# A list scheduler's rules and constants are rewritten, and a whole program is put in a new order

## The chip, the core and the metric

The kernel runs on one core of a Trainium2 chip. The core's engines each run their own queue of instructions in order: TensorE (PE in the profile, with its weight loads shown apart as PEld), VectorE (DVE), ScalarE (ACT), GpSimd (POOL) and SyncE (SP, which only issues DMAs here). An instruction that needs a value from another engine waits for a semaphore, and everything behind it on its own queue waits with it. The metric is device time in microseconds (us), from one launch to its end.

## The reference

A batch of 32 elements, each a 256 x 256 block in fp32, goes through four layers, one after another. Cut to what matters:

```
x = layer_0(x, t)        # conditioning vectors from t; two whole-block norms, silu, two 256x256 products, residual
x = layer_1(x, mask, timestep, bias)
    # norm, scale and shift; 16 heads of width 16: softmax(q k^T / 4 + bias, mask) v
    # output product, norm, 256 -> 1024 -> 256 feed-forward with x * sigmoid(1.702 x)
x = layer_2(x, A, B, dt) # finite differences along both axes of A*x and B*x, x + dt * df, max(., 0)
x = layer_3(x, gate)     # norm, 16 causal heads of width 16, feed-forward with exact gelu, gated residual
```

The attention bias alone is 32 x 16 x 256 x 256 floats; it is what the kernel mostly loads (512 DMAs of 256 KB).

## The kernel before

Each batch element is one block of 128 partitions x 2 x 256. Nothing depends on another batch element, so the work of several elements can be mixed on the engines: while one element is in its layer 3, the next is in layer 1 and the one after in layer 0.

The code of a layer does not issue instructions. `Order.record` only notes every operation with its operands, its nominal time `order.now`, and a cost from `Order.length`. `trace` sets the nominal time: element b's layer i starts at `b * PERIOD + START[i] + EDGE[b, i]`, each `yield` of a layer moves it on by that step's size times `PACE[i]`, and `SHIFT[i]` moves single steps to and fro. When all is recorded, `arrange` plays the program through on a model of the five engines: at each moment it gives every free engine the ready unit with the lowest rank (the nominal time, for PE less `EARLIER` of its tile's kind). The start times that come out are not used as times. `emit` issues all instructions sorted by them, so the model sets only the order of each queue; semaphores do the rest on the chip. As all instructions are issued by one line of `emit`, the profile names that line, L365 (`call(*args, **kwargs)`), for every one of them, and groups have to be told apart by their tiles.

What the model counts, in `length` and `arrange`:

- the length of each operation by engine, method and elements a partition (the pair returned is the time until its result is there and the time until the engine is free);
- `HOPS` and `OWNS`: from an operation's end to the start of a dependent one on another engine and on its own; `SLACK` is added where the dependent one is on PE;
- on PE, three array shapes: full 128x128, 32 rows x 128 (scores, tile `sc`: heads of width 16 in slots of 32 rows) and 128 x 32 columns (the products with the values, tile `pt` into `mm`). Each change of shape costs `TURN`, the first product of a slot `FIRST`, and `SEEN` is when a result counts as landed;
- a port that DVE and POOL are taken to share: an operation marked `x["port"]` starts only after the other engine's marked one is done;
- PSUM: eight banks, of which `CAPS` lets at most so many be used by scores (`sc`), transposed probabilities (`tr`) and everything else (`mm`).

PE works on six kinds of units: full fp32 products (256 columns; two records in the profile for each), transpositions through the identity (`ident`, one record), mean products of one column (`mean_mat`), stencil products of 129 columns, scores and value products. A unit of `order.together()` stays in one piece.

The steps that the prediction follows: `values` multiplies the transposed probabilities with V into `mm` and ACT copies it to `ctx_t`; `inverse_sums` has POOL spread the reciprocals of the softmax sums into `wide`; `normalise` has PE transpose `wide` and DVE multiply `ctx_t` by it; the product `ctx_t` x `L1wo` follows. `token_norm` has DVE take the statistics `st` and `mv`, `rstd_of` has POOL compute `rstd` (two small instructions, the second a power), DVE computes `shift` from it (128 x 2 elements), and ACT writes the normalised tile `t`, which PE transposes. POOL's largest work is `nb`: 512 subtractions of the attention bias from the mask, 16 for an element.

Of the kernel before, what the change touches and what calls it, by code (L numbers as in the profile page):

```python
# [21 lines left out]
P = 128  # L22
# [19 lines left out]
PERIOD = 86.0  # L42
START = (-59.8, 0.0, 116.9)
PACE = (1.37, 1.22, 1.08)
EDGE = {(0, 0): -102.4, (0, 1): -3.5, (0, 2): 0.3, (1, 0): -29.2, (1, 1): -9.5, (1, 2): -3.3, (2, 0): -4.4, (2, 1): -1.3, (2, 2): 1.9, (3, 0): 7.5, (3, 2): 0.7, (4, 0): -2.3, (4, 1): 1.2, (4, 2): 0.6, (27, 0): 7.3, (27, 1): 1.5, (27, 2): 0.7, (28, 0): -2.3, (28, 1): 1.6, (28, 2): 4.6, (29, 0): 2.1, (29, 1): -0.7, (29, 2): -0.1, (30, 0): 0.1, (30, 1): 3.4, (30, 2): -0.3, (31, 0): 3.1, (31, 1): 3.6, (31, 2): -30.9}
SHIFT = (
    {0: -23.5, 1: -31.5, 2: -24.4, 3: -36.5, 4: -13.4, 5: -35.7, 6: -44.8, 7: -28.5, 8: 20.9},
    {0: -11.9, 1: -93.5, 2: -5.9, 3: 2.4, 4: 4.1, 5: 6.4, 7: -9.2, 8: 7.3, 9: -92.1, 11: 7.2, 12: 20.9,
     13: -0.6, 14: 4.6, 15: -3.0, 16: 12.9, 17: 7.8, 19: 5.4, 20: 7.9, 21: 35.0, 22: 16.8, 23: -7.6,
     24: -11.1, 25: -25.5, 26: -3.5, 27: -66.1, 28: -0.5, 29: -110.6, 30: -4.3, 31: -15.2, 32: -19.4,  # L50
     33: 1.6, 34: -0.4, 35: 12.9, 36: 0.6, 37: -15.0},
    {0: -3.0, 1: -43.2, 2: 3.0, 3: 26.5, 4: 23.8, 5: -31.8, 6: -42.4, 7: -14.5, 8: -8.2, 9: 6.5,
     11: 3.8, 12: 16.4, 13: -29.4, 15: -3.4, 16: 18.0, 17: -4.1, 18: 7.0, 19: 0.1, 20: 0.7, 21: -69.9,
     23: 8.3, 24: 7.8, 25: -0.5, 26: -13.8, 27: -43.4, 28: 14.4, 29: -5.3, 30: 25.3, 31: 1.7, 32: -8.7,
     33: -40.0, 34: 13.4, 35: -21.0, 36: -92.3, 37: -36.5, 38: -60.7, 39: 56.2, 40: -26.9, 41: 7.7},
    {0: -11.5, 1: 3.4, 2: -31.6, 3: -95.1, 4: 57.5},
# [8 lines left out]
class Order:  # L65
# [9 lines left out]
    HOPS = {"act": 40.0, "dve": 40.0, "pool": 90.0, "pe": 60.0, "sync": 60.0}  # L75
    OWNS = {"act": 30.0, "dve": 30.0, "pool": 83.0, "sync": 30.0}
    TURN = 92.0
    FIRST = {(32, P): 107.0, (P, 32): 27.0}
    SLACK = 50.0
    SEEN = 165.0  # L80
    CAPS = {"sc": 6, "tr": 7, "mm": 6}
    EARLIER = {"sc": 28.7, "mm": -1.9, "tr": 6.1}
    STAY = 5.0
    PORT = 0.05
# [41 lines left out]
    def record(self, engine, call, method, args, kwargs):  # L126
# [12 lines left out]
        inner = [a for a in ins if math.prod(n for _, n in a.ap[1:]) >= 16]  # L139
        sources = sum(a.space != PSUM for a in inner)  # L140
        alone = method in ("tensor_scalar", "tensor_copy") and all(a.space != PSUM for a in outs)
        x["port"] = bool(inner) and (engine == "pool" or engine == "dve" and (sources > 1 or sources == 1 and alone))
# [25 lines left out]
    def length(self, engine, method, outs, ins, args, kwargs):  # L168
# [5 lines left out]
        if engine == "pe":  # L174
            lhs = kwargs.get("lhsT")
            rows = 32 if lhs is not None and lhs.partition_size() <= 32 else P
            cols = 32 if outs[0].partition_size() <= 32 else P
            slot = (lhs.start_partition(), outs[0].start_partition()) if lhs is not None else (0, 0)
            passes = 1 if method == "transpose" or kwargs.get("is_transpose") else 2
            one = max(free(outs[0]) / 1.2 + 2.3, 109.0) if free(outs[0]) > 16 else 70.0  # L180
            return one * passes, (rows, cols), slot
        if method == "dma_start":
            return sum(math.prod(k for _, k in a.ap) for a in outs) * 4
        if engine == "dve":
# [3 lines left out]
            if method == "tensor_tensor_reduce":  # L188
                return 235 + 1.05 * n, 73 + 1.05 * n, lead
# [3 lines left out]
            elif method == "scalar_tensor_tensor":  # L193
                a = 205 + 1.05 * n
                lead = 195.0
            else:
                a = 148 + 1.05 * n
            return a, a - 80, lead
        if engine == "act":
            if method == "copy":  # L200
                a = 157 + 0.84 * n
            else:
                a = (255 if columns else 200) + 0.84 * n + (93 if columns > 1 else 0)
                if "accum_out" in kwargs:
                    a += 115
            return a, a - 95, self.TABLES.get(args[2] if len(args) > 2 else None)
        if method == "tensor_tensor":
            a = 640 if n <= 4 else 185 + 2.13 * n
        else:
            a = 185 + 0.86 * n + (70 * columns if columns > 1 else 0)  # L210
        return a, a - 40 if n > 4 else a + 10

    def arrange(self):
# [48 lines left out]
        table = None  # L262

# [12 lines left out]
        while todo:  # L276
# [6 lines left out]
            for e in self.ENGINES:  # L283
# [6 lines left out]
                for k, heap in ready[e].items():  # L290
# [5 lines left out]
                    if e == "pe" and units[u][2][0]["length"][1] != shape:  # L296
                        rank += self.STAY
                    if k[1]:
# [11 lines left out]
                for x in units[u][2]:  # L310
                    if e == "pe":
                        one, its_shape, slot = x["length"]
                        if its_shape != shape:
# [7 lines left out]
                        done = t + one + (0.0 if slot in slots else self.FIRST.get(shape, 0.0))  # L321
# [3 lines left out]
                        done += self.SEEN  # L325
# [4 lines left out]
                    else:  # L330
                        x["start"] = now
                        more = max((pool_end if e == "dve" else dve_end) - now - x["lead"], 0.0) if x["port"] else 0.0
                        more = max([more] + [t - now for f, t in map(banks.__getitem__, x["banks"]) if f != e])
# [3 lines left out]
                        done, t = (now + a + more for a in x["length"][:2])  # L337
                        if x["port"] and e == "pool":
# [848 lines left out]
```

## Time and profile before

| what | number |
|---|---|
| median of 3 runs | 2708.8 us (2708.65 to 2711.2) |
| profiled execution, its own time | 2711.45 us |
| its span, first to last instruction | 2709.7 us |
| granted TensorE clock, mean over the span | 0.988 |
| PE busy | 2616.1 us, 97% |
| DVE, ACT, POOL busy | 80%, 71%, 58% |
| DMA | 169.67 MB, 63 GB/s over the span |

How to read it: a span is the stretch between two times; an engine is busy when an instruction of its own runs, and the busy time of PE contains waits that lie between two overlapping records, since a product's end is modelled. Start times are exact, so for PE this text counts from the start of one group to the start of the next. In a row of a timeline the columns are start, duration, engine, source line, operation, tiles (output <- inputs), shape and how many; in square brackets stands the idle time of the engine before it, and who ended it.

The program falls into a head, until the first element has passed its attention (about 96 us), a middle in which every element's work recurs in the same order, and a tail, in which the last elements have nothing beside them. From the 6th to the 24th element the same instruction returns every 81.3 us.

### The profile page before, as it was taken

The numbers are of one execution on the slowest core, as the hardware profiler recorded it, in microseconds if no ns is written. First come the engines' busy times: TensorE is split into PE (matmuls) and PEld (weight loads), VectorE is DVE, ScalarE is ACT, GpSimd is POOL, SyncE is SP. The second block draws the span as 40 slices with busy tenths as digits, with TensorE's granted clock in tenths as the row PEclk, the third lists the DMA queues.
The fourth block names the chain that finished last, engine by engine and source line by source line (L and its number), as shares of the span: only waits on it lengthen the run. The fifth ranks groups of instructions, "written<-read, shape, count | busy, mean of one in ns | idle before, by whom it ended". The sixth has DMA issues, their size and how long they took to land.

```text
span 2709.7 us, 60241 instructions
## 1 busy us (share of the span) xinstructions
PE 2616.1 (97%) x20462; PEld 2121.2 (78%) x20462; DVE 2166.8 (80%) x7499; ACT 1929.2 (71%) x6120; POOL 1570.6 (58%) x1960
## 2 busy tenths in 40 slices
PE   5999999999999999999999999999999999999987
PEld 3778788888788878788878788878787878888775
DVE  5887878888888888888888888888887887888753
ACT  1767777877767877767877767877777877777854
POOL 3855666555666555666555666555666555666420
PEclk7999999999999999999999999999999999999998
DMA  6411122211122211122211122211122211122100
GB/s 225 122 54 54 59 64 68 69 56 49 49 72 68 68 55 46 53 72 68 69 54 46 53 72 68 68 54 46 55 70 68 68 56 42 56 68 64 44 5 8
DMA packets 177062, 169.67 MB, mean 63 GB/s; under 512 B 19514, under 2 KB 175220, under 8 KB 176756
## 3 DMA queue, kind: packets, MB, share of 16 engines
q1 hardware_dynamic: 176720, 165.82, 19.9%
q8 instruction: 163, 2.67, 0.4%
q14 instruction: 143, 1.17, 0.1%
q10 hardware_dynamic: 36, 0.01, 0.0%
HBM read 157.40 MB, written 8.39 MB: 61 GB/s over the span
## 4 chain that ended last, share of the span: by engine, by line
PE 61%; POOL 25%; DVE 6%; issue 4%; ACT 2%; DMA 1%; SPq 0%; ACTq 0%; POOLq 0%; DVEq 0%
PE mm L365 45%; POOL nb L365 10%; PE tr L365 9%; PE sc L365 7%; POOL rstd L365 4%; POOL d L365 2%; POOL offset L365 2%; POOL mask_f L365 2%; DVE pr L365 1%; POOL cmf L365 1%; POOL b0f L365 1%; DVE st L365 1%; POOL a0f L365 1%; POOL cpf L365 1%; POOL small L365 1%
## 5 line engine op out<-in xcount | busy, mean ns | idle before, releaser
L365 ACT ACTIVATE pr<-pr,mn 128x256 f32<-128x256 f32 (+1 forms) x2048 | 967.9, 479 | 153.3 <-DVE mn L365 142.0
L365 POOL TENSOR_TENSOR nb<-mask_f,nb 128x512 f32<-128x512 f32 x512 | 683.9, 1355 | 60.7 <-DMA nb<-in_fside_Bx16xSxS_dram 46.6
L365 PE MATMUL tr<-ident,pr 128*128 128x128 f32 x3584 | 491.5, 275 | 8.1 <-ACT pr L365 2.5
L365 PEld LDWEIGHTS tr<-ident,pr 128*128 128x128 f32 x3584 | 416.4, 142 | 77.2 <-ACT pr L365 23.5
L365 DVE CUSTOM_DVE_ANT_0 pr<-sc,nb 128x256 f32<-128x256 f32 x1024 | 387.7, 417 | 90.0 <-PE sc L365 87.0
L365 ACT ACTIVATION_READ_ACCUMULATOR pr<-pr,mn 128x1 f32 x2048 | 397.1, 194 | 0.0
L365 DVE CUSTOM_DVE_ANT_0 pr<-sc,causal 128x128 f32<-128x128 f32 (+1 forms) x1024 | 309.5, 350 | 57.9 <-PE sc L365 40.7
L365 DVE COPY pt<-tr 128x512 f32<-128x512 f32 (+1 forms) x512 | 311.4, 615 | 45.8 <-PE tr L365 43.7
L365 POOL TENSOR_SCALAR hid<-hid 128x256 f32<-128x256 f32 x256 | 99.8, 405 | 373.1 <-ACT hid L365 372.9
L365 ACT COPY pt<-tr 128x512 f32<-128x512 f32 (+1 forms) x512 | 261.9, 528 | 56.6 <-PE tr L365 51.8
L365 POOL COPY wide<-rs 128x256 f32<-128x256 f32 x128 | 53.5, 418 | 414.5 <-DVE rs L365 384.4
L365 PE MATMUL sc<-k_t,nq 32*128 32x256 f32 (+1 forms) x4096 | 268.3, 374 | 0.0
L365 PE MATMUL mm<-h_t,L1w 128*128 128x256 f32 x1024 | 252.2, 386 | 0.7 <-DVE mn L365 0.4
L365 PE MATMUL mm<-h_t,L3w 128*128 128x256 f32 x1024 | 249.5, 388 | 1.8 <-DVE h_t L365 1.3
L365 PE MATMUL mm<-L3w,hid 128*128 128x256 f32 x1024 | 239.2, 387 | 10.2 <-ACT hid L365 10.2
L365 PE MATMUL mm<-L1w,hid 128*128 128x256 f32 x1024 | 243.4, 381 | 0.0
L365 PEld LDWEIGHTS mm<-L3w,hid 128*128 128x128 f32 x1024 | 193.2, 194 | 36.2 <-ACT hid L365 11.5
L365 PEld LDWEIGHTS sc<-k_t,nq 32*128 32x128 f32 x4096 | 162.5, 184 | 69.6 <-issue 27.8
L365 PEld LDWEIGHTS mm<-h_t,L3w 128*128 128x128 f32 x1024 | 188.7, 194 | 32.0 <-issue 6.1
L365 PEld LDWEIGHTS mm<-h_t,L1w 128*128 128x128 f32 x1024 | 182.7, 190 | 38.6 <-DVE pt L365 6.0
L365 PEld LDWEIGHTS mm<-L1w,hid 128*128 128x128 f32 x1024 | 184.9, 190 | 21.8 <-issue 1.6
L365 ACT ACTIVATE t<-x,shift,rstd 128x256 f32<-128x256 f32 x128 | 70.0, 593 | 160.6 <-DVE shift L365 160.2
(173 smaller groups left out, 5060.4 us busy)
## 6 DMA issues: line engine op xcount, KB each, us to landing
nb<-in_fside_Bx16xSxS_dram SPq DMA_DIRECT2D x512, 256.0 KB
x<-in_x_dram SPq DMA_DIRECT2D x32, 256.0 KB
out_dram<-d SPq DMA_DIRECT2D x32, 256.0 KB
mask<-in_mask_Bx1xSxS_bk_dram SPq DMA_DIRECT2D x32, 64.0 KB
L1w<-in_L_cond_W_dram SPq DMA_DIRECT2D x2, 1024.0 KB
L3w<-in_L_cond_W_dram SPq DMA_DIRECT2D x2, 1024.0 KB
l0w<-in_L_cond_W_dram SPq DMA_DIRECT2D x1, 1024.0 KB
g_b<-in_L_cond_B_grid_dram SPq DMA_DIRECT2D x3, 256.0 KB
```

Source lines behind the costliest of these rows:

```text
L365: call(*args, **kwargs)
```

## The change

No operation is added or taken out: both programs issue the same 12606 products on PE, and the same instructions on DVE, ACT and POOL. What changes is the model in `Order` and the nominal times, and with them the order on all five queues.

The rules:

- the port is now marked for operations of any size over one element a partition (it was 16 elements or more), with DVE's single-source `tensor_scalar` and `tensor_copy` only above 4;
- POOL's small operations get new lengths (`tensor_tensor` of n <= 4 columns 402 + 150 n ns, before 640; others 190 or 260), and `APART` keeps 120 ns between certain POOL operations;
- a value from PE is seen 165 ns after the product of a full or a score product, and 16 ns before the modelled end of a value product (before: 165 for all); `SLACK` ahead of PE goes from 50 to 200 ns;
- `FIRST` is also charged to the first full product (two passes) after a change of shape, and `FRESH` adds 8 us to the rank of such a product at that moment, so that a transposition is taken first if one is ready; `STAY` goes from 5 to 0;
- a few more lengths (small DVE operations with a reduction or a scalar, ACT with two columns of operands), `HOPS`, `OWNS`, `PORT`, `CAPS` (`sc` 6 to 8, `tr` 7 to 5, `mm` 6 to 7), `EARLIER`.

`PERIOD`, `START`, `PACE`, `EDGE` and `SHIFT` all get new values. The diff, with the rows of the tables left out:

```diff
--- before.py
+++ after.py
@@ -39,21 +39,22 @@
 
 
 
-PERIOD = 86.0
-START = (-59.8, 0.0, 116.9)
-PACE = (1.37, 1.22, 1.08)
-EDGE = {(0, 0): -102.4, (0, 1): -3.5, (0, 2): 0.3, ... }
+PERIOD = 86.1
+START = (-62.8, 0.0, 117.7)
+PACE = (1.4, 1.22, 1.09)
+EDGE = {(0, 0): -121.8, (0, 1): 3.6, (0, 2): -0.5, ... }
 SHIFT = (
...
 )
 NORM = 8.0
 LAND = 3.0
@@ -72,16 +73,19 @@
 
 
     SETUP = 15e3
-    HOPS = {"act": 40.0, "dve": 40.0, "pool": 90.0, "pe": 60.0, "sync": 60.0}
-    OWNS = {"act": 30.0, "dve": 30.0, "pool": 83.0, "sync": 30.0}
+    HOPS = {"act": 36.0, "dve": 36.0, "pool": 90.0, "pe": 54.0, "sync": 60.0}
+    OWNS = {"act": 34.0, "dve": 34.0, "pool": 83.0, "sync": 30.0}
     TURN = 92.0
-    FIRST = {(32, P): 107.0, (P, 32): 27.0}
-    SLACK = 50.0
-    SEEN = 165.0
-    CAPS = {"sc": 6, "tr": 7, "mm": 6}
-    EARLIER = {"sc": 28.7, "mm": -1.9, "tr": 6.1}
-    STAY = 5.0
-    PORT = 0.05
+    FIRST = {(32, P): 107.0, (P, 32): 27.0, (P, P): 107.0}
+    APART = 120.0
+    SLACK = 200.0
+    SEEN = {(32, P): 165.0, (P, 32): -16.0, (P, P): 165.0}
+    CAPS = {"sc": 8, "tr": 5, "mm": 7}
+    EARLIER = {"sc": 28.7, "mm": 1.7, "tr": 6.4}
+    STAY = 0.0
+    FRESH = 8.0
+    PAIR = 0.0
+    PORT = 0.02
     TABLES = {AF.Sin: 0, AF.Tanh: 1, AF.Exp: 1, AF.Gelu: 2}
     TABLE = 1300.0
     ENGINES = ("pe", "dve", "act", "pool", "sync")
@@ -136,10 +140,9 @@
         on_chip = lambda aps: [a for a in aps if a.space in (PSUM, bass.MemoryType.SB)]
         outs, ins = on_chip(outs), on_chip(ins)
 
-        inner = [a for a in ins if math.prod(n for _, n in a.ap[1:]) >= 16]
-        sources = sum(a.space != PSUM for a in inner)
-        alone = method in ("tensor_scalar", "tensor_copy") and all(a.space != PSUM for a in outs)
-        x["port"] = bool(inner) and (engine == "pool" or engine == "dve" and (sources > 1 or sources == 1 and alone))
+        inner = [n for n in (math.prod(n for _, n in a.ap[1:]) for a in ins if a.space != PSUM) if n > 1]
+        alone = method in ("tensor_scalar", "tensor_copy") and all(a.space != PSUM for a in outs) and max(inner, default=0) > 4
+        x["port"] = bool(ins) and (engine == "pool" or engine == "dve" and (len(inner) > 1 or len(inner) == 1 and alone))
         x["lead"] = 142.0 if engine == "pool" else x["length"][2] if engine == "dve" else 0.0
         x["banks"] = {a.tensor.name for a in ins + outs if a.space == PSUM} if engine != "pe" else set()
         at = (len(self.units), len(self.group) if self.group is not None else 0)
@@ -178,7 +181,7 @@
             slot = (lhs.start_partition(), outs[0].start_partition()) if lhs is not None else (0, 0)
             passes = 1 if method == "transpose" or kwargs.get("is_transpose") else 2
             one = max(free(outs[0]) / 1.2 + 2.3, 109.0) if free(outs[0]) > 16 else 70.0
-            return one * passes, (rows, cols), slot
+            return one * passes, (rows, cols), slot, passes
         if method == "dma_start":
             return sum(math.prod(k for _, k in a.ap) for a in outs) * 4
         if engine == "dve":
@@ -186,13 +189,13 @@
             if method == "reciprocal":
                 return 120 + 8.3 * n, 40 + 8.3 * n, lead
             if method == "tensor_tensor_reduce":
-                return 235 + 1.05 * n, 73 + 1.05 * n, lead
+                return 155 + 1.05 * n, 73 + 1.05 * n, lead
             if method == "tensor_scalar":
                 a = (265 if columns else 150) + (1.06 if psum else 0.55) * n
                 lead = 257.0 if columns else lead
             elif method == "scalar_tensor_tensor":
-                a = 205 + 1.05 * n
-                lead = 195.0
+                a = (205 if n > 4 else 155) + 1.05 * n
+                lead = 195.0 if n > 4 else lead
             else:
                 a = 148 + 1.05 * n
             return a, a - 80, lead
@@ -200,15 +203,17 @@
             if method == "copy":
                 a = 157 + 0.84 * n
             else:
-                a = (255 if columns else 200) + 0.84 * n + (93 if columns > 1 else 0)
+                a = (255 if columns else 200) + 0.84 * n + ((93 if psum else 123) if columns > 1 else 0)
                 if "accum_out" in kwargs:
                     a += 115
             return a, a - 95, self.TABLES.get(args[2] if len(args) > 2 else None)
+        numbers = {a for a in args if isinstance(a, float)}
+        apart = method == "tensor_scalar" and (len(numbers) == 2) + 2 * (len(numbers) == 1 and columns == 1)
         if method == "tensor_tensor":
-            a = 640 if n <= 4 else 185 + 2.13 * n
+            a = 402 + 150 * n if n <= 4 else 185 + 2.13 * n
         else:
-            a = 185 + 0.86 * n + (70 * columns if columns > 1 else 0)
-        return a, a - 40 if n > 4 else a + 10
+            a = (260 if apart == 2 else 190) if n <= 4 else 185 + 0.86 * n + (70 * columns if columns > 1 else 0)
+        return a, a - 40, apart
 
     def arrange(self):
 
@@ -260,6 +265,7 @@
         dma = pool_end = dve_end = 0.0
         banks = defaultdict(lambda: (None, 0.0))
         table = None
+        pool_free, apart = 0.0, 0
 
         def may(u, at):
             ready_at[u] = max(ready_at[u], at)
@@ -295,6 +301,10 @@
                         continue
                     if e == "pe" and units[u][2][0]["length"][1] != shape:
                         rank += self.STAY
+                        if units[u][2][0]["length"][1] != (P, P):
+                            rank -= self.PAIR if shape != (P, P) else 0.0
+                        elif units[u][2][0]["length"][3] == 2:
+                            rank += self.FRESH
                     if k[1]:
                         rank += self.PORT * max((pool_end if e == "dve" else dve_end) - now, 0.0)
                     if best is None or (rank, u) < best[0]:
@@ -309,8 +319,9 @@
                 t = end = now
                 for x in units[u][2]:
                     if e == "pe":
-                        one, its_shape, slot = x["length"]
-                        if its_shape != shape:
+                        one, its_shape, slot, passes = x["length"]
+                        turned = its_shape != shape
+                        if turned:
                             t = max(t, pe_end + self.TURN)
                             shape, slots = its_shape, {}
                         elif its_shape != (P, P):
@@ -318,11 +329,12 @@
                         else:
                             t = max(t, pe_end)
                         x["start"] = pe_last = t
-                        done = t + one + (0.0 if slot in slots else self.FIRST.get(shape, 0.0))
+                        begins = turned and passes == 2 if shape == (P, P) else slot not in slots
+                        done = t + one + (self.FIRST[shape] if begins else 0.0)
                         slots[slot] = done
                         pe_end = max(pe_end, done)
                         t = done if shape == (P, P) else t + 6.6
-                        done += self.SEEN
+                        done += self.SEEN[shape]
                     elif x["method"] == "dma_start":
                         x["start"] = now
                         dma = max(dma, now + 1700) + x["length"] / 330.0
@@ -330,11 +342,17 @@
                     else:
                         x["start"] = now
                         more = max((pool_end if e == "dve" else dve_end) - now - x["lead"], 0.0) if x["port"] else 0.0
+                        if e == "pool":
+                            if apart == 1 or x["length"][2]:
+                                more = max(more, pool_free + self.APART - now)
+                            apart = x["length"][2]
                         more = max([more] + [t - now for f, t in map(banks.__getitem__, x["banks"]) if f != e])
                         if e == "act" and x["length"][2] not in (None, table):
                             table = x["length"][2]
                             more += self.TABLE
                         done, t = (now + a + more for a in x["length"][:2])
+                        if e == "pool":
+                            pool_free = t
                         if x["port"] and e == "pool":
                             pool_end = done
                         elif x["port"]:

```

## The prediction

> **What bounds the kernel now.** I read the page first, then the stages by windows, then the waits of PE, then a timeline of one element in the middle.
>
> ```profile
> PE 2616.1 (97%) x20462; PEld 2121.2 (78%) x20462; DVE 2166.8 (80%) x7499; ACT 1929.2 (71%) x6120; POOL 1570.6 (58%) x1960
> ```
>
> PE is the bound. Its instructions are the same in both programs, so the change can win only time in which PE stands, or time that the order itself makes PE spend. The windows say where PE stands (span's start and end, length, then busy time of each engine with its count of records; the granted clock behind POOL's):
>
> ```profile
> 0.00:95.70 95.70, 56.78 (x410) 40.88 (x411) 60.97 (x217) 34.53 (x102) 46.25 (x64) 0.84 0.64 207
> 95.70:501.60 405.90, 399.83 (x3137) 324.08 (x3137) 331.23 (x1173) 297.83 (x955) 250.53 (x315) 1.00 0.20 60
> 501.60:1964.90 1463.30, 1444.29 (x11441) 1178.41 (x11440) 1220.76 (x4175) 1080.26 (x3432) 884.82 (x1098) 1.00 0.20 61
> 1964.90:2618.10 653.20, 647.25 (x5107) 527.22 (x5105) 519.09 (x1821) 479.06 (x1526) 372.54 (x462) 1.00 0.18 56
> 2618.10:2709.70 91.60, 67.92 (x373) 50.61 (x372) 34.75 (x117) 37.48 (x107) 16.45 (x22) 0.84 0.02 6
> ```
>
> PE is idle 38.9 us in the head, 19.0 in the middle (18 elements of 81.3 us), 23.7 in the tail, 12 elsewhere. The waits of PE name the middle's:
>
> ```profile
> PE mm L365 <- DVE ctx_t L365: 19.6, 19, 1.7
> ```
>
> One such wait, on PE, then what DVE and POOL do meanwhile:
>
> ```profile
> 1274.75 0.44 PE L365 MATMUL mm<-ident,wide 128*128 128x128 f32 x2
> 1275.02 3.62 PE L365 MATMUL mm<-L3w,hid 128*128 128x256 f32 x16
> 1278.50 0.38 PE L365 MATMUL mm<-dev,mean_mat 128*128 128x1 f32 x2
> 1278.74 0.68 PE L365 MATMUL mm<-L1wo,ctx_t 128*128 128x256 f32 x2
> 1280.46 0.70 PE L365 MATMUL mm<-L1wo,ctx_t 128*128 128x256 f32 x2 [1.03 <-DVE ctx_t L365]
> ```
> ```profile
> 1278.86 1.21 DVE L365 SCALAR_TENSOR_TENSOR shift<-mv,rstd 128x2 f32<-128x2 f32 x1 [0.41 <-POOL rstd L365]
> 1279.99 0.41 DVE L365 TENSOR_TENSOR ctx_t<-ctx_t,mm 128x256 f32<-128x256 f32 x1
> ```
> ```profile
> 1277.66 1.16 POOL L365 TENSOR_TENSOR rstd<-rstd,mhalf 128x2 f32<-128x2 f32 x1
> 1278.80 2.49 POOL L365 TENSOR_TENSOR nb<-mask_f,nb 128x512 f32<-128x512 f32 x2
> ```
>
> The reader should see this: `shift` works on two elements a partition. Its 128 records have a median of 160 ns; here it takes 1.21 us, as long as the `nb` that POOL began 0.06 us earlier. `ctx_t` is queued behind it, and PE's second output product for `ctx_t`. The old model did not count an operation of two elements as one that shares the port, so it planned 0.2 us for it. From the first to the second product lie 1.72 us where 0.43 are usual: 1.29 us lost.
>
> **The change, part by part.** No operation is added or removed; I counted both built programs' queues.
>
> *The wait for `ctx_t`.* In the new order of a middle element, PE does between `wide` and the second `L1wo` product one mean product (0.14), four transpositions of `x` (0.44), four products with `l_wout` (1.72), eight with `L3w` (3.45) and the first `L1wo` (0.43): 6.2 us, where the old has 1275.02 to 1278.74 and 0.43, 4.15 us. On DVE `shift`, the sum into `x`, and four statistics no longer stand in front of `ctx_t`, but `x<-x` (1.25) and `var` do. From the last transposition that feeds this queue, PE has 10.7 us of work until it needs `ctx_t`. DVE has, by its rows' durations less the 0.08 that neighbours overlap, two copies 1.2, `b1f` 1.66, three additions into `dd` 2.47, five small ones 0.49, `x` 1.07, `y` 0.63, `x` 1.16 and `ctx_t` 0.41: 9.1 us. So 1.6 us are left, and the wait should go: 19 x 1.29 = 24.5 us. What is behind the moved `shift` is ACT's `t` of the next element; its transposition keeps 0.17 us by the same kind of sum with `shift` at 1.21.
>
> *The wait for `h_t`.* Four products with `L1wq` take 1.92 us (1286.62 to 1288.54) instead of 1.73, and the first with `L3wq` 0.10 more, for DVE's `h_t`: 0.28 us, in 17 elements, 4.8 us. The new order puts 2.16 us of PE work between transposition and product instead of 1.72, so this goes too.
>
> *Changes of shape.* The prices on PE by start times:
>
> ```profile
> 1320.04 0.38 PE L365 MATMUL mm<-ident,wide 128*128 128x128 f32 x2
> 1320.26 1.89 PE L365 MATMUL mm<-L1w,hid 128*128 128x256 f32 x8
> 1321.99 0.60 PE L365 MATMUL tr<-ident,pr 128*128 128x128 f32 x4
> 1322.52 1.15 PE L365 MATMUL sc<-k_t,nq 32*128 32x256 f32 x16
> 1323.60 1.51 PE L365 MATMUL mm<-pt,L3v 128*32 128x256 f32 x32
> 1325.04 1.99 PE L365 MATMUL mm<-th,l_win 128*128 128x256 f32 x8
> 1326.87 1.89 PE L365 MATMUL mm<-L3wo,ctx_t 128*128 128x256 f32 x8
> ```
>
> Eight records of products take 1.73 us (1320.26 to 1321.99), but 1.83 straight behind a narrow shape (1325.04). Two transpositions take 0.22, but 0.28 behind scores (1312.36 to 1312.64). Four transpositions ahead of scores take 0.53 where 0.43 are usual. Over all such places the starts give 0.104, 0.056 and 0.093 us. In the old order PE leaves the narrow shapes 314 times: 156 times for a product, 158 for a transposition. In the new one 329: 63 and 266. That is 93 x -0.104 = -9.7, 108 x 0.056 = +6.0, and 15 more entries at 0.093 = +1.4 (leaving costs the same 0.11 whether another narrow shape follows or not): -2.3 us. So the rule for the first product mostly trades one price for another.
>
> The Trainium skill speaks against this part: "TensorEngine Tiling (Array Packing)", Key Properties, says that a change of tiling mode drains the array. The trace agrees that each change costs. By the constant of 166 ns in "TensorE: Matmul & The Clock Gate", Single matmul latency, 15 more changes would be an estimated 2.5 us instead of 1.4; no row here shows so much.
>
> *New waits in the middle.* Over a middle element I summed for each wait of PE what its producer's queue, and the queue that feeds this, must do in time. The old order misses at `ctx_t` and at `t` by 0.4 to 0.7 us (the chip lost more, so such sums are a lower bound). The new misses nowhere; the tightest are the mean product for `dev` (0.12 us), `L1wv` behind ACT's `k_t` (0.15) and `t` (0.17). One `nb` lasts 1.27 or, beside DVE, 1.71 us in this stretch: 0.44 later is 0.3 missed. I take 0.3 us an element, 18 x 0.3 = +5.4, with ends 0 and 24 (one `ctx_t`-like wait of 1.3 us in each).
>
> *Head.* Element 0's first scores start at 63.9 us, behind two one-column products of element 1 that waited (1.5 us in front of `mv`). The new order puts these behind the scores, and the third pair of `nb` before POOL's work for element 1; SP loads it before the 2 MB of `L3w` instead of after. But the fourth needs a buffer that the first scores free, and DVE has grid set-up work in front of `shift`. I expect the element's output product 2 us earlier, with 1.8 us less of PE's work done by then (38.1 of 39.9): 0, with ends -4 and +5 (POOL's stand from 57.4 to 62.7 us won or lost). Its granted clock of 0.84 should stay.
>
> *Elements 24 to 31.* The same sums miss by up to 0.7 to 2.3 us in five stretches, where the old order's miss in two. +2 us, from 0 to +6.
>
> *Tail.* The last layer 1 ends with 54.2 us of PE's work to come, instead of 51.0: 3.2 us earlier. But 41.3 us instead of 39.7 follow the start of its layer 3. The serial chain between (11.2 us to the stencil, then 13.2 to `t`) is the same. -2 us, from -3.2 to 0.
>
> SP's DMAs are the same 662 issues; DMA engines are 20% busy in the middle, so their new places cost nothing unless a buffer of `nb` is freed late, which is in the sums through DVE.
>
> Sum: -24.5 - 4.8 - 2.3 + 5.4 + 0 + 2 - 2 = -26.2 us. The profiled execution's own time is 2711.45 (span 2709.7 and 1.75 around it), 2.65 above the median of 2708.8. So 2685.3 against the one, 2682.6 against the other: 2684.
>
> **Rivals.** *Everything goes.* The margins hold, the late elements gain as the middle does, and the remaining small waits (0.2 us an element) go: -5.4 - 2 - 4.4 on top, about 2672. For it: the new lengths are the rows' own (POOL's power on two columns 0.70 us back to back, planned 0.64 before, 0.702 now). Against it: POOL's rows scatter by 0.4.
>
> *The wait moves on.* In the chain of waits from 1270 to 1280 us nearly all is POOL (`cmf`, `offset`, `nb`, `rstd`), ending in `shift` and `ctx_t`. If POOL's `rstd` is late again for another product, the 29.3 us return: about 2707, no change. Against it: POOL is busy 885 of 1463 us in the middle.
>
> *Slower, through the transposition banks.* `CAPS` leaves 5 banks for `tr`. Between a transposition and the reuse of its bank lay a median of 3.0 us of PE's work where DVE empties it; now 1.5, and 1.19 at least. From transposition to emptied bank take 0.86 to 1.17 us. A copy that stands behind one port-blocked operation (1.2 us longer) makes PE stand about 0.9 to 1.2. It decides from 0.9 us an element (30 x 0.9 = 27, all of the gain); at 1.2 the time is 2684 + 36 = 2720. For it: the least margin falls. Against it: 1.5 is still over 1.17.
>
> **How the numbers follow.** A measurement tells about 0.2% (5.4 us) from no change. The forecast has 0.50, its own range 2675 to 2694; everything goes 0.20; the wait moves on 0.10; the banks 0.15; a head, late elements and a tail worse by all the ends of these parts (2695) 0.05. Faster is the forecast, the first rival and the last: 0.75, and a little of the second, 0.76; same 0.08; slower 0.16. The range leaves out about 1 in 10 on each side: 2662 to 2714.
>
> **What would show it.** Right: the period in the middle falls from 81.3 to about 80.0 us; no row of PE waiting for `ctx_t`; transpositions follow most scores. Wrong: the same period with another tile in that row; waits of PE for `pt` in front of `tr`; a head over 100 us.

## The result, and the profile after

The median of four runs is 2690.26 us (2688.96 to 2691.16) against 2709.39 us (2708.65 to 2711.2) for the kernel before, run beside it: a ratio of 0.9928, 95% interval 0.9911 to 0.9945. The forecast was 2684 with a range of 2662 to 2714. The profiled execution took 2690.35 us (span 2688.6), 21.1 us less than the one before; the forecast's sum for it was -26.2.

The stages by windows, cut at the same times as before (the last row ends with the span); columns as in the prediction:

```profile
0.00:95.70 95.70, 60.85 (x412) 43.58 (x412) 58.04 (x215) 34.09 (x101) 45.20 (x62) 0.84 0.64 204
95.70:501.60 405.90, 392.23 (x3016) 317.91 (x3014) 329.80 (x1124) 283.73 (x901) 247.70 (x309) 0.98 0.20 60
501.60:1964.90 1463.30, 1461.46 (x11690) 1198.11 (x11683) 1204.93 (x4261) 1101.97 (x3533) 893.91 (x1112) 1.00 0.20 62
1964.90:2618.10 653.20, 642.53 (x5025) 523.69 (x5025) 535.54 (x1808) 467.31 (x1487) 375.23 (x470) 0.99 0.17 53
2618.10:2688.60 70.50, 53.73 (x333) 39.80 (x331) 22.84 (x95) 35.20 (x101) 5.79 (x9) 0.93 0.02 8
```

In the middle row PE is idle 1.8 us where it was idle 19.0, and does 249 records more in the same 1463.3 us. The row above it is the surprise: 13.7 us idle where there were 6.1, a granted clock of 0.98 instead of 1.00, and 121 records less. The middle won, the stretch before it lost.

The waits of PE by cause, in us, times and longest. First those of the whole span, then all that there are between 501.6 and 1964.9 us:

```profile
PE mm L383 <- ACT t L383: 9.1, 3, 3.9
...
PE mm L383 <- DVE th L383: 8.3, 2, 4.8
PE mm L383 <- ACT hid L383: 7.4, 4, 4.2
```
```profile
PE mm L383 <- DVE rows_t L383: 1.6, 4, 0.5
PE mm L383 <- DVE dev L383: 0.2, 1, 0.2
```

The row of waits for `ctx_t` (17 of its 19 lay there) is gone from the middle; two of together 0.3 us are left, both in the head. Outside the middle other waits have grown, those for `h_t` from 1.5 us (3 times) to 4.8 us (9 times). A middle element, by the timelines of PE, DVE and POOL:

```profile
1275.75 3.62 PE L383 MATMUL mm<-L3w,hid 128*128 128x256 f32 x16
1279.20 1.03 PE L383 MATMUL mm<-L1wo,ctx_t 128*128 128x256 f32 x4
```
```profile
1275.73 0.42 DVE L383 TENSOR_TENSOR ctx_t<-ctx_t,mm 128x256 f32<-128x256 f32 x1 [0.42 <-ACT ctx_t L383]
...
1281.21 0.16 DVE L383 SCALAR_TENSOR_TENSOR shift<-mv,rstd 128x2 f32<-128x2 f32 x1 [2.74 <-POOL rstd L383]
```
```profile
1271.97 6.92 POOL L383 TENSOR_TENSOR nb<-mask_f,nb 128x512 f32<-128x512 f32 x5
```

`ctx_t` is finished at 1276.15 us; its second product starts at about 1279.6, 3.5 us later. POOL works through five `nb` first, `shift` comes behind them and runs alone, in 0.16 us, and `ctx_t` no longer stands behind it. Over the whole program 32 of the 128 `shift` began while an `nb` ran before (median 1.21 us), 8 do after. From the 6th to the 24th element the same instruction returns after 79.73 us in most of them (81.3 before).

To see where PE stands I took, for each of its records, the time to the next start, less the median for a record of its kind between such neighbours, and summed what is over 25 ns (columns: stretches of the span in us; the last one to the end):

| kernel | 0-81 | 81-163 | 163-488 | 488-1951 | 1951-2520 | 2520-end | sum |
|---|---|---|---|---|---|---|---|
| before | 39.8 | 11.6 | 7.3 | 34.0 | 11.7 | 38.3 | 142.7 |
| after | 39.7 | 23.0 | 7.3 | 10.2 | 10.8 | 31.2 | 122.3 |
| `shift_behind` | 37.8 | 11.8 | 6.7 | 26.7 | 11.9 | 35.9 | 130.8 |
| `shift_single` | 40.7 | 11.6 | 5.3 | 14.2 | 8.4 | 33.8 | 114.0 |
| `product_first` | 41.2 | 22.8 | 8.4 | 13.1 | 10.8 | 34.0 | 130.3 |
| `port_old` | 41.9 | 21.4 | 9.1 | 9.7 | 20.8 | 36.6 | 139.4 |
| `b2_early` | 41.1 | 17.8 | 7.2 | 8.6 | 12.7 | 33.0 | 120.5 |
| `head_all` | 40.2 | 16.8 | 4.4 | 9.4 | 10.8 | 30.1 | 111.6 |
| `all_starts` | 42.8 | 16.4 | 4.4 | 8.4 | 7.3 | 31.8 | 111.1 |

How far such a number can be trusted is seen in `after`, `b2_early` and `head_all`: behind 549 us their traces have the same order on PE, DVE, ACT and POOL, and yet they stand 10.8, 12.7 and 10.8 us between 1951 and 2520 us and 31.2, 33.0 and 30.1 us behind. So a difference of 2 to 3 us in one column can be scatter.

The change won 23.8 us of standing in the middle, 7.1 in the tail and 0.9 ahead of it, and lost 11.4 us between 81 and 163 us. This is where the loss lies, on PE:

```profile
150.55 3.78 PE L383 MATMUL mm<-l_wout,th 128*128 128x256 f32 x8 [4.78 <-DVE th L383]
154.12 0.42 PE L383 MATMUL mm<-dev,mean_mat 128*128 128x1 f32 x2
155.99 1.18 PE L383 MATMUL mm<-ident,t 128*128 128x128 f32 x4 [1.44 <-ACT t L383]
157.81 3.78 PE L383 MATMUL mm<-h_t,L3wq 128*128 128x256 f32 x8 [0.64 <-DVE h_t L383]
161.39 1.06 PE L383 MATMUL mm<-ident,t 128*128 128x128 f32 x4
162.24 2.30 PE L383 MATMUL mm<-h_t,L3wk 128*128 128x256 f32 x8
```

Element 2's layer 0 is late: its first product (`th` x `l_win`) starts at 128.8 us, before at 94.8. PE stands 4.78 us for its `th`. And then the clock is down. By windows of about 3.4 us, cut where the granted clock changes (135.8, 139.2, 149.4 and 163.1 us) and evenly between; the granted clock is the number behind POOL's busy time:

```profile
132.40:135.80 3.40, 1.48 (x14) 1.27 (x12) 3.40 (x10) 0.62 (x2) 3.31 (x4) 0.99 0.00 0
135.80:139.20 3.40, 3.40 (x18) 3.40 (x18) 2.88 (x12) 2.80 (x10) 3.32 (x4) 0.51 0.09 19
...
146.00:149.40 3.40, 0.00 (x0) 0.00 (x0) 3.40 (x5) 0.63 (x1) 3.40 (x3) 1.00 0.00 0
149.40:152.80 3.40, 2.25 (x5) 1.85 (x6) 2.97 (x9) 0.00 (x0) 3.21 (x6) 0.50 0.00 0
152.80:156.30 3.50, 2.06 (x8) 1.64 (x6) 1.93 (x8) 0.96 (x2) 2.48 (x4) 0.50 0.00 0
156.30:159.70 3.40, 2.76 (x9) 1.82 (x8) 1.89 (x9) 1.52 (x4) 1.79 (x4) 0.50 0.00 0
159.70:163.10 3.40, 3.40 (x12) 2.77 (x11) 1.47 (x4) 1.30 (x4) 1.41 (x2) 0.51 0.27 77
163.10:166.50 3.40, 3.40 (x23) 2.76 (x25) 0.44 (x1) 1.44 (x4) 0.00 (x0) 1.00 0.00 0
```

Eight records of `l_wout` take 3.57 us from start to start and eight of `L3wq` 3.58, where 1.73 is usual; the transpositions and `L3wk` behind them lose another 0.8. So three waits (4.8 + 1.4 + 0.6 = 6.8) came with 4.5 us of slow clock, together about what the stretch lost; all else that stands in it comes to 11.7 us, where the kernel before had 11.6. (That rest is not the same: it holds another hole, of 1.92 us up to 134.8 us, which had put the clock down for one window already.)

### The profile page after: what moved, and what is told of

The parts are those of the page before. It is cut to its first block, busy times and chain, and to the rows that moved or that the text cites. A ratio compares the mean times of both kernels' runs of the same rounds, so it can differ in the third digit from the quotient of the medians.

```text
span 2688.6 us, 60251 instructions
## 1 busy us (share of the span) xinstructions
PE 2610.8 (97%) x20462; PEld 2123.1 (79%) x20462; DVE 2151.1 (80%) x7499; ACT 1922.3 (71%) x6120; POOL 1567.8 (58%) x1960
## 4 chain that ended last, share of the span: by engine, by line
PE 86%; DVE 5%; POOL 4%; ACT 2%; DMA 2%; issue 1%; SPq 0%; ACTq 0%; POOLq 0%; DVEq 0%
PE mm L383 64%; PE tr L383 13%; PE sc L383 8%; POOL nb L383 1%; DMA nb<-in_fside_Bx16xSxS_dram 1%; ACT pr L383 1%; DVE pr L383 1%; DVE o L383 1%; DVE pt L383 1%; POOL d L383 0%; DVE st L383 0%; POOL rstd L383 0%; SPq L383 0%; POOL b0f L383 0%; ACT L383 0%
## 5 line engine op out<-in xcount | busy, mean ns | idle before, releaser
L383 PE MATMUL tr<-ident,pr 128*128 128x128 f32 x3584 | 505.8, 276 | 7.8 <-ACT pr L383 3.5
L383 PEld LDWEIGHTS tr<-ident,pr 128*128 128x128 f32 x3584 | 410.9, 141 | 106.4 <-ACT pr L383 33.1
L383 DVE CUSTOM_DVE_ANT_0 pr<-sc,nb 128x256 f32<-128x256 f32 x1024 | 381.2, 416 | 86.0 <-PE sc L383 47.6
```

## Experiments

Undo the clash in three ways, take the change apart, price one of its rules by itself, and repair the head. Each was timed beside the kernel before, whose median was 2710.2 to 2710.4 us there.

**One swap in the old order: `shift_behind`.** In `emit`, after sorting:

```diff
+        for x, y in zip(dve, dve[1:]):
+            if uses(x, "shift") and uses(y, "ctx_t") and y["start"] < x["start"] + 300.0:
+                i, j = xs.index(x), xs.index(y)
+                xs.insert(j, xs.pop(i))
```

> The kernel before, and nothing moved but 17 of the 19 `shift` that stand straight in front of `ctx_t` on VectorE: each changes place with it. All other queues are the same to the instruction. If the forecast's mechanism is right (1.29 us of TensorE time for each), 17 x 1.29 = 21.9 us go: 2687 us, and the same instruction returns every 80.0 us in the middle instead of 81.3. If the wait only moves on to the normalised tile `t`, which needs `shift` (now begun 0.4 us later, still beside a subtraction of `nb`), TensorE waits for `t` instead, up to 1.2 us in each element: 2700 to 2709 us, period above 80.8.

2701.8 us (2699.7 to 2705.3), ratio 0.997 (0.996 to 0.998): 8.4 us less, and a period of 80.9. The rival has the larger part. PE's waits, and one place on DVE and ACT:

```profile
PE mm L373 <- ACT t L373: 24.1, 25, 3.7
...
PE mm L373 <- DVE ctx_t L373: 2.0, 2, 1.7
```
```profile
1272.37 0.40 DVE L373 TENSOR_TENSOR ctx_t<-ctx_t,mm 128x256 f32<-128x256 f32 x1
1272.86 1.22 DVE L373 SCALAR_TENSOR_TENSOR shift<-mv,rstd 128x2 f32<-128x2 f32 x1
```
```profile
1274.11 1.09 ACT L373 ACTIVATE t<-x,shift,rstd 128x256 f32<-128x256 f32 x2 [4.84 <-DVE shift L373]
```

The wait for `ctx_t` is gone from the middle and one for `t` stands in its place: `shift` collides as before, only later, and `t` needs it. (Before, PE's waits for `t` were 8, together 12.2 us.) To move the victim is worth a third of the price; what has to go is the collision.

**The collision alone: `shift_single`.** The old order, every queue as it was; at the issue of `shift`:

```diff
+            if call == self.stt and x["tiles"] and any(t.source_name == "shift" for t in x["tiles"]):
+                shift, mean, _, r = args[:4]
+                for c in range(2):
+                    self.ts(shift[:, c : c + 1], mean[:, c : c + 1], r[:, c : c + 1], -1.0, ALU.mult, ALU.mult)
+                continue
```

> The kernel before, all queues in its own order, but each of the 128 `shift` (one instruction on two columns, two operands from SBUF) is issued as two instructions on one column each, with the reciprocal deviation as a scalar operand. This measures the clash by itself. In the profiled execution 34 of the 128 last 1.21 us beside a subtraction of `nb`, while `dev`, one column with a scalar operand, lasts 0.27 us beside `nb` and 0.27 us alone. If two elements a partition from two operands are what collides: two rows of about 0.26 us (0.45 together) instead of 1.21, 0.76 us less in front of `ctx_t`, 19 x 0.76 = 14.4 us, and up to 4 more where `t` waits for `shift`: 2692 to 2696 us. If any small instruction with an SBUF operand that comes between waits for the port: 1.4 us or more together, 2710 to 2715.

2684.4 us (2682.5 to 2685.7), ratio 0.9897 (0.9873 to 0.992): 26.0 us less than before, without any new order, and by the medians 6 us under the whole change. The tile's view of this run (minimum, median and maximum in ns), and the same place as above on DVE and POOL:

```profile
L368 DVE TENSOR_SCALAR shift<-mv,rstd x256: 195/205/216, 53.2 to 2650.1; 128x1 f32<-128x1 f32 x128
```
```profile
1267.81 0.33 DVE L368 TENSOR_SCALAR shift<-mv,rstd 128x1 f32<-128x1 f32 x2 [0.41 <-POOL rstd L370]
1268.06 0.41 DVE L370 TENSOR_TENSOR ctx_t<-ctx_t,mm 128x256 f32<-128x256 f32 x1
```
```profile
1267.74 2.68 POOL L370 TENSOR_TENSOR nb<-mask_f,nb 128x512 f32<-128x512 f32 x2
```
```profile
PE mm L370 <- ACT t L370: 8.1, 6, 3.8
...
PE mm L370 <- DVE ctx_t L370: 3.1, 9, 1.7
```

POOL's `nb` began 0.07 us earlier and runs on, yet the two instructions take 0.33 us together, 0.25 of it in front of `ctx_t`, where one took 1.21. The period is 80.2 us. It did better than expected. In the middle, counted as in the table, the standing between the output products fell from 22.1 to 7.1 us, by 15.0, as expected (14.4). Beside it fell what PE stood for `h_t`, from 4.8 to 1.1 us, which the expectation had left out; the waits for `t` went from 12.2 to 8.1 us over the span; and 9.8 us of the gain lie in the stretches ahead of and behind the middle (table: 2.0, 3.3 and 4.5).

**The same in the new order: `single_after`.** The same lines in the kernel after:

```diff
+            if call == self.stt and x["tiles"] and any(t.source_name == "shift" for t in x["tiles"]):
...
```

> The same replacement in the kernel after. There 9 `shift` still last 0.94 us or more beside `nb`, and 25 last 0.47 us beside POOL's sums into `x`. If in the new order nothing on TensorE waits for `shift` any more: within 2 us of after (2690). If `shift` still sets when TensorE goes on: 9 x 0.76 = 6.8 us less, 2683.

2690.6 us (2689.3 to 2692.2), no difference to after, and a period of 79.73 again. The new order had already taken `shift` off the path; the collisions that are left cost nothing that the time shows. (They are fewer than the expectation says: in the trace of after 6 `shift` last 0.94 us or more, not 9, and the 25 beside the sums into `x` last 0.15 to 0.68 us, with a median of 0.47.)

**Half the change: `rules_only` and `tables_only`.** The new `Order` with PERIOD, START, PACE, EDGE and SHIFT of before, and the old `Order` with the new tables:

```diff
-PERIOD = 86.1
-START = (-62.8, 0.0, 117.7)
+PERIOD = 86.0
+START = (-59.8, 0.0, 116.9)
...
```
```diff
-PERIOD = 86.0
-START = (-59.8, 0.0, 116.9)
+PERIOD = 86.1
+START = (-62.8, 0.0, 117.7)
...
```

> The new rules and constants of the planner with all the old tables of nominal times (PERIOD, START, PACE, EDGE, SHIFT). `shift` stands in front of `ctx_t` in 8 places instead of 19, so 11 x 1.29 = 14.2 us of that wait go, and by the prices of the changes of shape (88 products and 245 transpositions first, 332 exits) 0.4 us more. If the rules carry the gain by themselves: 2690 to 2697 us. If the tables are fitted to the rules, the order falls apart at other places: 2720 us or more, with waits of several different tiles in every element.

> The old rules and constants with the new tables. `shift` stands within three places in front of `ctx_t` 10 times instead of 19. If the tables carry the gain: 2685 to 2698 us. If rules and tables only fit together: 2720 us or more, as for the rules alone.

2759.1 us, ratio 1.0183 (1.0169 to 1.0197), and 2772.8 us, ratio 1.0233 (1.0219 to 1.0247): each alone is slower than before, by 49 and 63 us. The waits of PE between 501.6 and 1964.9 us, of the rules alone and of the tables alone:

```profile
PE mm L382 <- ACT ctx_t L382: 6.3, 4, 1.7
PE mm L382 <- ACT hid L382: 3.4, 6, 0.8
```
```profile
PE mm L366 <- DVE dev L366: 9.6, 5, 2.0
PE mm L366 <- DVE mn L366: 4.5, 5, 1.2
```

The wait for `ctx_t` behind `shift` is small in both (0.3 us at most, or none in the rows), and others are there, of several tiles; elements no longer recur alike (from the 6th to the 24th element the first output products are 79.5 to 86.0 us apart with the rules alone, 71.3 to 96.3 us with the tables alone). Here the nominal times belong to the costs that they were found with.

**The port rule alone taken back: `port_old`.** The kernel after with the old mark:

```diff
-        inner = [n for n in (math.prod(n for _, n in a.ap[1:]) for a in ins if a.space != PSUM) if n > 1]
+        inner = [a for a in ins if math.prod(n for _, n in a.ap[1:]) >= 16]
+        sources = sum(a.space != PSUM for a in inner)
...
```

> The kernel after with one rule taken back: the port is marked as before, for operations of 16 or more elements a partition. In this order `shift` stands within three places in front of `ctx_t` 3 times (2 in after, 19 in before), and the changes of shape are 329, 61 of them for a product. If the new tables of nominal times keep `shift` out of the way by themselves: a period of 79.7 us in the middle as in after, and 2688 to 2696 us. If the rule is what kept small operations off POOL's long ones: a wait of 1 us in most elements again, period 80.5 or more, 2705 us or more.

2710.1 us (2705.7 to 2712.2), ratio 1.000 (0.9991 to 1.0008): all of the gain is gone, but for neither reason given. The period in the middle is 79.78 us and 9 `shift` begin while an `nb` runs; with these tables the middle needs no port rule. The 18 us are lost at the ends: 10.0 us of standing more between 1951 and 2520 us, 5.4 in the tail, 2.4 ahead of 488 us. The waits of PE over the span:

```profile
PE mm L384 <- ACT hid L384: 15.8, 7, 5.2
PE mm L384 <- ACT t L384: 15.3, 6, 5.9
```

against 7.4 us in 4 and 9.1 in 3 after. The traces show that the one mark has reordered the end: of 2497 places in which PE's queue differs from that of after, 1913 lie behind 2000 us. Why this order of the last elements is the worse one was not followed further.

**The price of the shape rule: `product_first`.** In 203 places of the kernel after, one product goes in front of the transpositions that follow a narrow block:

```diff
+                if m > k and full(pe[m]) and pe[m]["length"][0] > 300.0:
+                    deps = [self.units[u][2][i] for u, i in pe[m]["deps"]]
+                    if all(at[id(d)] < at[id(pe[k])] for d in deps):
+                        before.setdefault(id(pe[k]), pe[m])
```

> The kernel after with one move on TensorE in 203 places: where a block of scores or value products is followed by transpositions and these by a full product, the first product goes in front of the transpositions. Exits to a product become 264 instead of 61, exits to a transposition 63 instead of 266; all other queues are unchanged. By the prices of the profile before (0.104 us for the first product, 0.056 for the first transposition) this costs 203 x 0.048 = 9.7 us: 2700. If the prices are not real costs of the order: 2690, no change. If the transpositions, 0.43 us later each time, make TensorE stand for what follows from them: 2705 or more, with new waits for `pt` or `pr`.

2710.3 us (2705.2 to 2712.0), 20 us over after; the profiled span is 2706.1 us, 17.5 over. One exit of each kernel, on PE (this one, then after):

```profile
1303.13 0.94 PE L403 MATMUL sc<-k_t,nq 32*128 32x128 f32 x16
1304.00 0.70 PE L403 MATMUL mm<-h_t,L1w 128*128 128x256 f32 x2
1304.54 0.82 PE L403 MATMUL tr<-ident,pr 128*128 128x128 f32 x6
1305.19 0.60 PE L403 MATMUL mm<-h_t,L1w 128*128 128x256 f32 x2
1305.77 0.41 PE L403 MATMUL tr<-ident,pr 128*128 128x128 f32 x2
```
```profile
1299.94 0.94 PE L383 MATMUL sc<-k_t,nq 32*128 32x128 f32 x16
1300.81 0.88 PE L383 MATMUL tr<-ident,pr 128*128 128x128 f32 x6
```

Two records of the first product last 0.54 us from start to start, where 0.43 is usual, in 261 such places: the median of a first record is 320 ns against 216, as in both other kernels, and that of a first transposition 165 against 109. By these prices the changes of shape cost 61.8 us instead of 52.0, 9.7 more, as expected, and the standing is 8.0 us more (table), together 17.7; so close a match is partly luck, given the scatter of the table. So the prices are real, and the order that the rule gives is worth it.

In the middle the standing has a cause of its own. Two places in each element, behind the moved product, make a transposition late: in the rows above the one at 1305.77 comes about 0.14 us later than the 0.43 us of the product allow. In all 37 such places of the middle, 4.5 us together, the transposition starts 0.135 us after the end of DVE's copy of an earlier one, and all that it can want of this copy is the bank of PSUM that it frees. Here the copy is, on DVE,

```profile
1305.07 0.56 DVE L403 COPY pt<-tr 128x384 f32<-128x384 f32 x1
```

which ends at 1305.63. These gaps are too short to be rows of waits. They are the third rival of the prediction, the wait for a transposition bank, in a small form and in another kernel than the change.

**The head: `b2_early` and `head_all`.**

```diff
-(2, 0): 19.2
+(2, 0): -29.8
```
```diff
-(0, 0): -121.8, (0, 1): 3.6, (0, 2): -0.5, (1, 0): 6.3, (1, 1): 0.6, (1, 2): 1.2, (2, 0): 19.2
+(0, 0): -135.2, (0, 1): 2.0, (0, 2): -10.2, (1, 0): 4.8, (1, 1): -0.6, (1, 2): -0.7, (2, 0): -31.5
...
```

The first diff is `b2_early`, the second `head_all`, both in EDGE of the kernel after.

> The kernel after with one number changed: the nominal start of element 2's layer 0 (EDGE) 49 us earlier, -29.8 instead of 19.2. The kernel after stands on TensorE 23.0 us in its second stretch of 81.3 us, where the kernel before stands 11.6; the longest wait there is 4.8 us for `th` of element 2's layer 0, and 1.4 and 0.6 us follow behind it. If this late layer 0 is what the head lost: 4 to 7 us less than after, about 2685 us, and no wait for `th` over 1 us between 100 and 170 us. If the hole only stands for a lack of other ready work (element 0 is in its serial chain of layer 2, element 1 has no scores yet), another wait takes its place and the time stays within 2 us of after, 2690.

> The kernel after with other nominal starts (EDGE) for the layers of elements 0 to 4: element 2's layer 0 by -50.7 us, the others by -13.4 to +9.9. Element 2's layer 0 alone brought 3.0 us of the 11.4 that the head lost, and 17.8 us of standing are left in its second stretch. If the head's loss is a matter of these starts: 2682 to 2686 us. If the rest is the chain of element 0 through layers 2 and 3, in which too little other work is ready: 2687 to 2690.

2687.3 us (2686.7 to 2687.7) and 2682.2 us (2678.1 to 2684.4); ratios to before 0.9917 (0.9904 to 0.9931) and 0.9889 (0.9865 to 0.9913). The interval of the first overlaps that of after, so its 3.0 us rest on the medians and the trace: no wait for `th` over 1 us is left there, `l_wout` runs at 133.56, and the standing from 81 to 163 us falls by 5.2, of which 3.4 come back elsewhere. The rows of PE:

```profile
133.56 1.89 PE L383 MATMUL mm<-l_wout,th 128*128 128x256 f32 x8
...
146.37 1.22 PE L383 MATMUL mm<-L1wo,ctx_t 128*128 128x256 f32 x2 [1.50 <-DVE ctx_t L383]
...
152.81 2.17 PE L383 MATMUL mm<-ident,t 128*128 128x128 f32 x8 [2.76 <-ACT t L383]
```

Both theories hold in part: the late layer was a cause, and shorter waits of the same stretch (`ctx_t`, `t`) come into view once it is early. What comes back elsewhere in `b2_early` lies behind 1951 us (3.7 in the table), where its queues are those of after: scatter. The other starts brought 5 us more. Against after, `head_all` stands 8.6 us less ahead of 488 us. But between 81 and 163 us it still stands 16.8 us: of the 11.4 lost there 6.2 came back, and for the other 5.2 no run shows the cause.

**Beyond both: `all_starts`.** New values in EDGE (elements 0 to 5 and 25 to 31) and SHIFT of the kernel after; of EDGE, for one:

```diff
-(0, 0): -121.8, (0, 1): 3.6, (0, 2): -0.5, (1, 0): 6.3, (1, 1): 0.6, (1, 2): 1.2, (2, 0): 19.2
+(0, 0): -103.6, (0, 1): 3.8, (0, 2): -7.9, (1, 0): 5.2, (1, 1): -0.5, (1, 2): -0.8, (2, 0): -16.5
...
```

> The kernel after with new nominal times (EDGE of elements 0 to 5 and 25 to 31, SHIFT of the layers), found by trying small changes in the planner's own model, whose end falls by 11.7 us against after; for the kernel with the starts of elements 0 to 4 changed it fell by 5.2, and the chip gave 8. If the model's ends go on to the chip: 2676 to 2681 us. If the remaining time lies in what the model leaves out (the granted clock of the head, the scatter of POOL): 2682 us, as with the starts of elements 0 to 4 alone.

2677.3 us (2672.8 to 2677.5), ratio 0.9872 (0.9857 to 0.9887): faster than before by 33 us and than after by 13. The planner's end fell by 11.7. Its middle is that of after (79.73); what it gained lies in the stretches up to 488 us and from 1951 to 2520 (6.4 and 3.5 us in the table, the second near its scatter).

## Why the prediction was right, and where not

- **The bound and the mechanism: right.** PE standing behind DVE's `shift`, held by POOL's `nb`. `shift_single` takes the collision away and leaves every queue's order as it was, and gets 26.0 us; `single_after` gets nothing more, so the new order had won the same thing. By the table 19.8 us of `shift_single`'s gain lie in the middle, where the forecast gave the two waits 28.0 (18 x 1.29 + 4.8).
- **Wait for `ctx_t` (-24.5) and for `h_t` (-4.8), new waits +5.4: right in the mechanism, each size somewhat too large.** For the 18 elements between 488 and 1951 us these terms make 18 x 1.29 + 4.8 - 5.4 = 22.6 us; the standing fell by 23.8. No row of either wait is left there, the period is 79.73 (forecast 80.0), and the margin at `ctx_t` is 3.5 us instead of the 1.6 of the sums, which had `b1f` at 1.66 us where it now takes 0.83. New waits are only 1.8 us in named rows, on `rows_t` and `dev`; so the two waits gave about 25.6 of their 28.0 us, and the two errors nearly cancel.
- **Changes of shape (-2.3): right, as far as the runs show.** The counts were known from the built programs; the prices are the same after (320 and 165 ns, as before), and `product_first` shows that moving exits from one kind to the other costs what they say. By them, 52.0 us after and 54.3 before: -2.2.
- **Head (0, from -4 to +5): wrong, and the step that failed is its end.** It was summed only as far as element 0's output product. That part came as said: the product starts at 92.7 us instead of 95.7, at a granted clock of 0.84. But the pipeline is not full at 96 us. Element 2's layer 0, which the new EDGE begins 20.8 us later, had been part of the filler for the stretch from 96 to 163 us, where element 0 is in its serial chain; there 11.4 us were lost, where the term was 0 and its worst end +5. No sum of queues was made for that stretch. With other starts 6.2 of the 11.4 came back (`head_all`); the cause of the rest stays open.
- **Elements 24 to 31 (+2, from 0 to +6):** -0.9, just outside; within the scatter of the table that is no change. The misses that the sums gave were not there.
- **Tail (-2, from -3.2 to 0): right in sign, too small: -7.1.** The sum had the earlier start of 3.2 us, and held the serial chain equal. Before, PE waited 4.15 us for `hid` of the last feed-forward but one and eight of its records took 3.2 us instead of 1.73; after, those products stand among the last element's attention and wait for nothing (before, then after):

```profile
2639.31 3.39 PE L365 MATMUL mm<-L3w,hid 128*128 128x256 f32 x8 [4.15 <-ACT hid L365]
```
```profile
2624.74 1.03 PE L383 MATMUL mm<-h_t,L3wk 128*128 128x256 f32 x4
2625.79 1.99 PE L383 MATMUL mm<-L3w,hid 128*128 128x256 f32 x8
```

- **The sum.** -23.8 - 2.2 + 11.4 - 0.9 - 7.1 = -22.6, 1.5 more than the 21.1 that the span lost; I did not trace the rest, which lies in differences under 25 ns. Against -26.2, the head's +11.4 is the miss, and the tail gave back 5. That the whole came so near is in part luck: the head and the tail both lie outside their ends, on opposite sides.
- **The rivals.** "The wait moves on" is what `shift_behind` does, not the change: in after POOL's `rstd` is in time. (Its 2707 us do not follow from its condition either: 29.3 us back on 2684 are 2713.) "Everything goes" is right for the middle alone. The transposition banks did not decide: in the middle of after no transposition waits, though five banks are allowed instead of seven. `product_first` shows that the wait exists, with 0.10 to 0.14 us in two places of an element.

## What to carry to other kernels

When a small instruction is long in some places only, look at what the other engine does at that moment, and first try to write it so that it cannot collide; that took 26 us with a few lines, where a new order of the whole program took 19. A planner's nominal times and its costs are one thing: neither half of this change was worth anything alone, and one rule taken back lost everything at the ends while the middle stayed. Sum the start of a pipeline up to the element from which the period holds, not to its first milestone, and count a hole with the slow clock that can follow it: here it followed already on one of 1.9 us that stood behind transpositions.

## What the runs showed of the hardware

A VectorE instruction on two elements a partition with two SBUF operands was held as long as GpSimd's subtraction beside it: 1.21 us for 0.16, and mostly 0.44 to 0.69 us beside the shorter sums into `x` (0.73 us). The same arithmetic on one column with a [128, 1] scalar operand was not held: 0.205 us, never over 0.216 in 256 records, 65 of which began while an `nb` ran. Which of the differences does it (one column, one operand as a scalar, another instruction) no run separates. The Trainium skill ("SBUF — State Buffer", Who interferes with whom) says that a VectorE instruction with two SBUF inputs contends with a GpSimd one that reads SBUF, and names no size from which on; these runs agree, down to two elements.

The granted clock of TensorE changed in steps of about 3.4 us or multiples of that (135.8, 139.2, 149.4, 163.1 us). In the kernel after, a window in which PE was busy 1.48 of 3.4 us and one in which it was idle were followed by 0.50. At 0.50, windows with 2.25, 2.06 and 2.76 us busy were followed by 0.50 again, and the two that were busy throughout by 1.00. Waits of up to 1.0 us in the middle of the kernel before left it at 1.00. The Trainium skill ("TensorE: Matmul & The Clock Gate", Part 1: The HAM clock gate) says that an idle window of some 3.4 us halves the clock, that a busy one of that length restores it, and that the windows run freely, not from the start of the work. The trace agrees on the length and on the busy window: the 3.6 us of `l_wout` products from 150.5 us on filled no window and restored nothing. On the idle one it goes further: the window from 132.4 us on was not idle throughout (transpositions, a hole of 1.92 us, then stencil products) and had the same effect. How busy a window must be, these few do not tell.
